# Two more split products, quarter products begun ahead of the half product in front of them, and one more bias sum added by transfers, in a two-layer cross-attention kernel

## The chip, the cores and the metric

The kernel runs on one core of one Trainium2 chip. Its time is the device time of one execution in microseconds; the time given is the median of several. A core has a matrix engine, TensorE (PE in the profile), and three engines for elementwise work: VectorE (DVE), ScalarE (ACT) and GpSimd (POOL). SyncE (SP) issues most of the DMA transfers. Each engine has its own queue of instructions and works through it in order; semaphores make one engine wait for another. PE writes its results to banks of PSUM, a small memory from which ACT and DVE fetch them; all else is in SBUF.

## What is computed

Two layers of cross-attention, all in float32. The queries come from x (8 sequences of 100 tokens of 1024), the keys and values of both layers from one context (8 times 1444 rows of 512). Cut to what matters:

```
# layer 0
Q = x @ Wq + bq ; K = ctx @ Wk + bk ; V = ctx @ Wv + bv
w = softmax(Q @ K.T / sqrt(1024), over the 1444 context rows)
x = x + (w @ V) @ Wo + bo
# layer 1, with weights of its own
q = x @ Wq + bq ; k = ctx @ Wk + bk ; v = ctx @ Wv + bv
w = softmax(q @ k.T / sqrt(1024), over the 100 tokens)
y = w @ v + x
out = layer_norm(y) * gamma + beta
```

## The kernel before

**Products of weights.** Keys and values are never made. Since Q·Kᵀ = x·(Wq·Wkᵀ)·ctxᵀ plus terms of the biases, the kernel first multiplies weights with weights (`weight_products`, L318): Wq·Wkᵀ of layer 0 ("qk0", 1024 to 512), then Wv·Wo of layer 0 ("vo0"), and after the queries of layer 0 Wq·Wkᵀ of layer 1 ("qk1"). `queries(layer)` (L584) multiplies these by x and gives the queries in the context's 512 features: "g0" and "g1". The stages in PE's order are qk0, vo0, g0, qk1, the scores (`s`, L786) and weighted sums of context rows (`A`, L757) of layer 0, the projection "o" by Wv·Wo, g1, scores and sums of layer 1, the projection by Wv, and the layer norm.

**Seven products.** Each of these matrix products is made in the way of Strassen and Winograd: both operands are cut into quarters (A11, A12, A21, A22 and B11 to B22), sums of them are formed on DVE (S1 to S4, T1 to T4), and seven half-size products take the place of eight. The seven are written to banks called X, Z, Y and W: X = A11·B11, Z = A12·B21, Y = S1·T1, then X += S2·T2, W = A22·T4, then X += S3·T3 with S3 = A11 − A21 and T3 = B22 − B12 (its matmuls, taken one at a time, are "V" in the code), and last Y += S4·B22 with S4 = A12 − S2. Between these, `put` copies a bank into the result (on ACT) and `add` adds a bank to it (on DVE). S3, T3 and S4 are written over A21, B12 and A12, so each such sum must wait until the last reader of the old contents is done.

**Inner products.** `inner_product` (L252) makes one of the seven in the same way once more, as seven quarter products in tiles named `.._x`, `.._z`, `.._y`, `.._w`. It forms four sums at once (S1, T1, A21 −, B12 −), and then two more sums behind each of the first two quarter products; later quarters read these. Before the change the products "w" (W) and "q" (the last one, Y += S4·B22) of vo0 and of qk1 are made so, and "w" of g0 and of g1; in qk0 none is.

**What sets the order.** PE's instructions keep the order of the program text (`manual_schedule`, L66). DVE's do so only where `vector.in_order` is set; elsewhere a scheduler orders them, as it does for ACT, except where `keep_in_program_order` is called. In vo0 and qk1 quarters of "w" alternate with pieces of V: after each quarter comes an eighth of V. After the loop comes the rest of V, then `add(1, 0, X)` and `add(1, 1, X)`, four additions of 128x512 from PSUM on DVE, and then all seven quarters of q.

**Bias sums.** The biases of keys, queries and values enter as sums over the rows of a weight matrix, each row scaled by an element of the bias (`accumulate`, L354). Where the rows are 1024 wide this is done for vo0 (bv) and qk1 (bk) by `transferred_sum` (L505): ACT scales the eight chunks into eight tiles (L510), and seven DMA transfers that add what they move to what lies at their destination (L514, issued by POOL) sum them up in three levels. In qk0 the sum for bk is made on DVE, by one scaling and seven multiply-adds of 128x1024. Readers of these sums are `block_sums` (a transpose and a reduction on DVE), called for qk0 within vo0 by `between`.

**Buffers.** Rows of the weights lie in `unit` tiles (ten, loaded by SP, released when the last product that reads them is done); `row` and `wT` tiles have three buffers each, `gT` three, and the three `prob` tiles stay.

Of the kernel before, what the change touches and what calls it, by code (L numbers as in the profile page):

```python
# [25 lines left out]
F32 = mybir.dt.float32  # L26
# [29 lines left out]
def two_layer_cross_attention(ctx: ExitStack, tc: tile.TileContext, a: dict, out: bass.AP):  # L56
# [26 lines left out]
    def weight_rows(name):  # L83
        return work.tile([P, MC * T + QD * (-(-T // QD)) - T], F32, tag="wT", name=name, bufs=3)

# [166 lines left out]
    def inner_product(name, lhs, rhs, nb, width, t, put, add):  # L252
# [18 lines left out]

        combine(S1, A21, A22, ALU.add)
        combine(T1, B12, B11, ALU.subtract)
        combine(A21, A11, A21, ALU.subtract)
        combine(B12, B22, B12, ALU.subtract)
# [4 lines left out]
        def steps():  # L280
            X = bank(f"{name}_x")
            product(X, A11, B11, True)
            put(0, 0, X)
            combine(B11, B22, T1, ALU.subtract)
            combine(A11, S1, A11, ALU.subtract)
            yield
            Z = bank2(f"{name}_z")
            product(Z, A12, B21, True)
            add(0, 0, Z)
            combine(B21, B21, B11, ALU.subtract)  # L290
            combine(A12, A12, A11, ALU.subtract)
            yield
            Y = bank(f"{name}_y")
            product(Y, S1, T1, True)
            put(1, 1, Y)
            yield
            product(X, A11, B11, False)
            put(0, 1, X)
            yield
            W = bank2(f"{name}_w")  # L300
            product(W, A22, B21, True)
            put(1, 0, W)
            yield
            product(Y, A12, B22, False)
            add(0, 1, Y)
            yield
            product(X, A21, B12, False)
            add(1, 1, X)
            add(1, 0, X)
            yield  # L310
# [7 lines left out]
    def weight_products(name, left, right, l_width, r_width, scaled, between=None):  # L318
# [35 lines left out]
        def accumulate(side):  # L354
            for v, of in scaled:
# [5 lines left out]
                if width == E and name != "qk0":  # L361
                    accs[v] = transferred_sum(f"{name}_{v}", srcs)
                    continue
                if width == E:
                    acc = row(f"{name}_{v}")
                else:
                    acc = work.tile([P, L], F32, tag="half", name=f"{name}_{v}", bufs=1)
# [67 lines left out]
        product(X, A11, B11, True)  # L435
        put(0, 0, X)
        combine(T1, B12, B11, ALU.subtract)
        if name == "qk0":
# [11 lines left out]
            product(W, A22, T4, True)  # L450
            put(1, 0, W)
        else:
# [3 lines left out]
            if not early:  # L456
                accumulate(1)
# [3 lines left out]
        put(1, 1, Y)  # L461
        if name != "qk0":
            vector.in_order = True
# [4 lines left out]
        S2 = S1  # L468
        if name != "qk0":
            combine(T4, B21, T2, ALU.subtract)  # L470
        combine(B12, B22, B12, ALU.subtract)
        product(X, S2, T2, False)
        put(0, 1, X)
        if name == "qk0":
            accumulate(0)
        combine(A21, A11, A21, ALU.subtract)
        if name == "qk0":
            combine(A12, A12, S2, ALU.subtract)
            product(X, A21, B12, False)
            add(1, 0, X)  # L480
            add(1, 1, X)
            product(Y, A12, B22, False)
            add(0, 1, Y)
        else:

            V = half_steps(X, A21, B12, False, nb, rh)
            t = work.tile([P, LC, GT], F32, tag="gT", name=f"{name}_t", bufs=3).rearrange("p c t -> p (c t)")
            for n, _ in enumerate(inner_product(f"{name}_w", A22, T4, nb, rh, t[:, :768], *parts(1, 0))):
                run(islice(V, 2 * nb // 4))
                if n == 2:  # L490
                    combine(A12, A12, S2, ALU.subtract)
                    add(0, 1, Y)
                elif n == 3:
                    _, more = parts(0, 1)
                    Q = inner_product(f"{name}_q", A12, B22, nb, rh, t[:, 768:1536], more, more)
                    if between:
                        between()
            run(V)
            add(1, 0, X)
            add(1, 1, X)  # L500
            run(Q)
            vector.in_order = False
        yield dst, [accs[v] for v, _ in scaled]

    def transferred_sum(name, srcs):  # L505

        tiles = [row(f"{name}_{n}") for n in range(2)] + [weight_rows(f"{name}_{n}")[:, :E] for n in range(2, 5)]
# [76 lines left out]
    def queries(layer, w, u):  # L584
# [41 lines left out]

        def steps():
# [4 lines left out]
            Z = pair("z")  # L632
            product(Z, A12, B21, True)
            vector.in_order = True
            combine(S1, A21, A22, ALU.add)
            combine(T1, B12, B11, ALU.subtract)
            combine(S2, S1, A11, ALU.subtract)
            combine(T2, B22, T1, ALU.subtract)
            vector.in_order = False
            yield  # L640
            vector.in_order = True
            add(0, 0, Z)
            combine(A21, A11, A21, ALU.subtract)
            combine(T3, B22, B12, ALU.subtract)
            Y = pair("y")
            product(Y, S1, T1, True)
            put(1, 1, Y)
            combine(T1, B21, T2, ALU.subtract)
            combine(A12, A12, S2, ALU.subtract)
# [6 lines left out]
            t = unit(f"g{layer}_w_t")  # L656
            V = half_steps(X, A21, T3, False, nb, GT)
            for _ in inner_product(f"g{layer}_w", A22, T1, nb, GT, t, *parts(1, 0)):
                next(V)
# [5 lines left out]
            product(Y, A12, B22, False)  # L665
# [426 lines left out]
    for n in range(5):  # L1092
        next(steps)
        if n == 0:
            kb1 = [key_bias_sums(f"kb1_{g}", g * GT, (g + 1) * GT, wqbk1) for g in range(B // G)]
# [60 lines left out]
```

## Time and profile before

| | us |
|---|---|
| Median of 3 runs | 639.41 (639.32 to 640.49) |
| The profiled execution | 639.97 |
| Its span | 638.2 |
| PE's busy time in it | 625.4 |
| VectorE's | 467.0 |
| ScalarE's | 157.2 |
| GpSimd's | 92.9 |

The span is what the hardware profiler saw between the first and the last instruction; the execution is 1.77 us longer. The granted clock of TensorE was 0.996 of full speed in the mean. Where a timeline is shown below, a line gives the start, the time up to the end of the last of a run of like instructions, the engine, the line of the program, the operation, what is written and read, the shape, and the number of instructions. What is in brackets is the time for which the engine had been idle, and who ended it. Ends on PE are modelled and overlap the next start, so times of products are taken from start to start. A float32 matmul of the program appears as two records.

The same page cuts the span into 40 slices of 16 us. Its rows on VectorE, on the granted clock and on the DMA engines, in tenths, are:

```profile
DVE  2993699976883797766655579539786659898886
...
PEclk9999999999999999999999999999999999999998
DMA  8948875015779888999965306156898890599002
```

The four stages of the change lie in slices 0 to 11 (qk0, vo0, g0 and qk1, up to 188.9 us) and in slices 24 to 27 (g1, from 385.8 to 433).

### The profile page before, as it was taken

What the parts mean: (1) busy time and instruction counts of PE and PEld (TensorE: products, weight loads), DVE (VectorE), ACT (ScalarE), POOL (GpSimd) and SP (SyncE); (2) the same over time, 40 slices, a digit from 0 to 9 for tenths busy, and PEclk for the clock granted to TensorE, in tenths of its full rate; (3) what the DMA queues carried; (4) which work ended last, traced back from release to release, by engine and by line L of the source; (5) the groups of instructions that cost most, each with busy time, mean ns of one, the idle gap of its engine ahead of it and who ended that gap; (6) DMA issues with size and microseconds to landing.
All of it is one profiled execution on the core that took longest, in us unless ns stands there. A gap on an engine that the chain in (4) does not pass through costs nothing.

```text
span 638.2 us, 10286 instructions
## 1 busy us (share of the span) xinstructions
PE 625.4 (98%) x4064; PEld 527.6 (83%) x4064; DVE 467.0 (73%) x912; ACT 157.2 (25%) x369; POOL 92.9 (15%) x124
## 2 busy tenths in 40 slices
PE   9999998999999999999999999999999999999994
PEld 8886465678985999999998655656999999999992
DVE  2993699976883797766655579539786659898886
ACT  1012410105203344223330000213432340325301
POOL 3000210001300000000000001007211220454054
PEclk9999999999999999999999999999999999999998
DMA  8948875015779888999965306156898890599002
GB/s 274 356 161 306 164 214 195 0 47 99 151 229 388 293 304 295 324 310 320 305 221 184 111 1 230 46 171 207 274 309 296 309 321 34 194 323 338 29 19 85
DMA packets 50933, 134.64 MB, mean 211 GB/s; under 512 B 4226, under 2 KB 8578, under 8 KB 50886
## 3 DMA queue, kind: packets, MB, share of 16 engines
q1 hardware_dynamic: 46792, 120.85, 55.5%
q0 software_dynamic: 3696, 12.68, 8.4%
q8 instruction: 32, 0.52, 0.3%
q10 hardware_dynamic: 398, 0.47, 0.2%
q14 instruction: 15, 0.12, 0.1%
HBM read 123.36 MB, written 3.28 MB: 198 GB/s over the span
## 4 chain that ended last, share of the span: by engine, by line
PE 91%; DVE 6%; issue 1%; POOL 1%; POOLq 0%; ACT 0%; DVEq 0%
PE s L786 25%; PE A L757 24%; PE qk_x L160 6%; PE g_x L160 5%; PE o_x L160 5%; PE g_y L160 3%; PE qk_y L160 3%; PE o_y L160 3%; DVE vo L93 3%; PE qk_z L160 2%; PE g_z L160 2%; PE o_w L160 2%; PE o_z L160 2%; DVE qk L93 2%; PE vo_x L160 1%
## 5 line engine op out<-in xcount | busy, mean ns | idle before, releaser
L757 PE MATMUL A<-w,c 120*128 120x100 f32 (+1 forms) x1536 | 247.7, 265 | 0.0
L757 PEld LDWEIGHTS A<-w,c 120*128 120x128 f32 (+1 forms) x1536 | 215.9, 190 | 0.8
L93 DVE STREAM_TRANSPOSE w<-prob 32x384 f32<-32x384 f32 (+1 forms) x256 | 143.6, 561 | 35.1 <-ACT prob L798 15.7
L786 PE MATMUL s<-cT,g1T 128*100 128x131 f32 (+2 forms) x592 | 122.9, 296 | 0.3 <-DVE g1T L93 0.3
L786 PE MATMUL s<-cT,g0T 128*100 128x131 f32 (+2 forms) x592 | 122.7, 296 | 0.0
L786 PEld LDWEIGHTS s<-cT,g1T 128*100 128x100 f32 x592 | 78.3, 167 | 9.3 <-DVE g1T L93 1.2
L786 PEld LDWEIGHTS s<-cT,g0T 128*100 128x100 f32 x592 | 78.3, 167 | 8.3
L798 ACT ACTIVATE prob<-s,c 100x393 f32<-100x393 f32 (+2 forms) x64 | 35.1, 561 | 114.4 <-PE s L786 114.1
L908 ACT ACTIVATE w<-w,negmax 120x100 f32<-120x100 f32 (+1 forms) x96 | 34.8, 365 | 82.3 <-DVE negmax L93 82.3
L818 DVE TENSOR_REDUCE maxima<-prob 100x1 f32<-100x394 f32 (+3 forms) x32 | 16.5, 528 | 25.5 <-ACT prob L798 25.3
L1105 POOL DMA_DIRECT2D wv<-in_L_xattn_Wv x1 | 0.8, 772 | 204.9 <-PE o_x L160 204.9
L160 PE MATMUL qk_x<-qk 128*128 128x256 f32 x128 | 29.9, 385 | 0.0
L927 POOL TENSOR_TENSOR part<-w 120x500 f32<-120x500 f32 x8 | 10.9, 1363 | 112.9 <-DVE rstd L1002 28.6
L160 PEld LDWEIGHTS qk_x<-qk 128*128 128x128 f32 x128 | 23.9, 194 | 3.2 <-ACT qk L409 0.2
L93 DVE TENSOR_TENSOR xT<-xT,o_x 128x400 f32<-128x400 f32 (+1 forms) x32 | 16.0, 541 | 6.4 <-PE o_x L160 6.1
L600 ACT ACTIVATE g1T<-g_x,k 128x400 f32<-128x400 f32 x4 | 2.4, 594 | 64.0 <-PE g_x L160 63.8
L908 ACT ACTIVATION_READ_ACCUMULATOR w<-w,negmax 120x1 f32 (+1 forms) x96 | 18.0, 187 | 0.0
L1007 POOL TENSOR_TENSOR z<-z,vectors 100x1024 f32<-100x1024 f32 x7 | 16.5, 2360 | 8.2 <-ACT z L1006 8.2
L985 PE MATMUL z<-ident,xT 128*100 128x128 f32 x64 | 16.3, 273 | 0.0
L93 DVE TENSOR_TENSOR w<-w,rtotal 120x400 f32<-120x400 f32 (+1 forms) x24 | 15.6, 650 | 0.7
L1006 ACT ACTIVATE z<-z,rstd 100x1024 f32<-100x1024 f32 x7 | 8.0, 1150 | 31.9 <-POOL rstd L1003 31.9
L989 DVE SCALAR_TENSOR_TENSOR z<-vectors,r,z 100x512 f32<-100x512 f32 x16 | 11.8, 741 | 4.9 <-PE z L985 4.8
(309 smaller groups left out, 932.5 us busy)
## 6 DMA issues: line engine op xcount, KB each, us to landing
cT<-in_ctxT SPq DMA_DIRECT2D x64, 722.0 KB, 6.4
c<-in_ctx SPq DMA_DIRECT2D x48, 768.0 KB, 8.2
c<-in_ctx SPq DMA_DIRECT2D x16, 512.0 KB, 6.8
vo<-in_L_xattn_Wo SPq DMA_DIRECT2D x8, 512.0 KB, 5.9
qk<-in_L_xattn_WqT SPq DMA_DIRECT2D x8, 512.0 KB
qk<-in_L_xattn_WqT SPq DMA_DIRECT2D x15, 256.0 KB, 5.8
c<-in_ctx SPq DMA_DIRECT2D x16, 224.0 KB, 5.7
xT<-in_xT SPq DMA_DIRECT2D x2, 1600.0 KB
```

What stands on the lines that cost most here:

```text
L93: ins = getattr(nc.vector, op)(*args, **kw)
L160: nc.tensor.matmul(banks[n // per][:, n % per * width : (n % per + 1) * width], lhs[i][:, n * P : (n + 1) * P], rhs[i], start=(fresh and i ...
L757: nc.tensor.matmul(ps[:, k * T : (k + 1) * T], c[m // CQ][:r, m % CQ, k * P : (k + 1) * P], w[:r, m, :], start=(m == 0 and k == 0), stop=( ...
L786: nc.tensor.matmul(banks[n // per][:T, cuts[n] - o : cuts[n + 1] - o], q[:, k, t0 : t0 + T], cT[k][:, cuts[n] : cuts[n + 1]], start=(k == ...
L798: nc.scalar.activation(p[:, part], ps[:T, : part.stop - part.start], AF.Identity, bias=key_bias[layer][:T, b : b + 1], scale=SCALE,)
L818: nc.vector.tensor_reduce(maxima[:, n : n + 1], p[:, part], AX.X, ALU.max)
L908: nc.scalar.activation(w[:r, m0 + m, :], w[:r, m0 + m, :], AF.Exp, bias=negmax[:r, m : m + 1], accum_out=total[:r, m : m + 1])
L927: add(part, w[:MR, 0:5, :], w[:MR, 5:10, :], ALU.add)
L985: nc.tensor.transpose(ps[:T, e * P : (e + 1) * P], xT[:, 4 * j + e, b * T : (b + 1) * T], ident)
L989: nc.vector.scalar_tensor_tensor(z[:, half], bv1[j][:T], s["r"], ps[:T, :], ALU.mult, ALU.add)
L1006: nc.scalar.activation(z, z, AF.Copy, scale=rstd)
L1007: nc.gpsimd.tensor_tensor(z, z, beta[:T], ALU.add)
```

## The change

In **qk0** the bias sum for bk is made by `transferred_sum` too, with other tiles (three `row`, one `wT`, one `gT`, three `prob`), ahead of the copy of W. The last product becomes an inner product "q".

In **qk0, vo0 and qk1** q's first quarter product is issued before the last part of V: in qk0 after half of V, in the others before V's last eighth. The four additions of X go from before q to behind its fifth quarter product. B12 − and, in vo0, A21 − are formed earlier, before T2. In vo0 ACT's scalings for bv go ahead of the copy of X, and DVE keeps the program's order from there on.

In **g1** the product Z becomes an inner product "z", behind Y instead of ahead of it; S4 is written over A11 and the room of T3 serves as room for z's sums. In g0 S4 is formed ahead of T4. `inner_product` gets an argument for where its right-hand sums go. The call of the key bias sums of layer 1 comes four steps later in the text.

```diff
@@ -83,6 +83,9 @@
     def weight_rows(name):
         return work.tile([P, MC * T + QD * (-(-T // QD)) - T], F32, tag="wT", name=name, bufs=3)
+    def wide_sums(name):
+        return work.tile([P, LC, GT], F32, tag="gT", name=name, bufs=3).rearrange("p c t -> p (c t)")
     class Vector:
@@ -249,7 +252,8 @@
         add(0, 1, Y)
         yield
-    def inner_product(name, lhs, rhs, nb, width, t, put, add):
+    def inner_product(name, lhs, rhs, nb, width, t, put, add, right=None):
@@ -269,10 +273,13 @@
         B11, B21, B12, B22 = quarters(rhs, width)
         S1, T1 = room(lhs, t[:, : 2 * h * P]), room(rhs, t[:, 2 * h * P : 2 * h * P + 2 * w])
+        T2, T3, T4 = B11, B12, B21
+        if right:
+            T1, T2, T3, T4 = right
         combine(S1, A21, A22, ALU.add)
         combine(T1, B12, B11, ALU.subtract)
         combine(A21, A11, A21, ALU.subtract)
-        combine(B12, B22, B12, ALU.subtract)
+        combine(T3, B22, B12, ALU.subtract)
         def product(ps, left, right, fresh):
             half_product([ps], left, right, fresh, h, w)
@@ -281,30 +288,30 @@
             X = bank(f"{name}_x")
             product(X, A11, B11, True)
             put(0, 0, X)
-            combine(B11, B22, T1, ALU.subtract)
+            combine(T2, B22, T1, ALU.subtract)
             combine(A11, S1, A11, ALU.subtract)
             yield
             Z = bank2(f"{name}_z")
             product(Z, A12, B21, True)
             add(0, 0, Z)
-            combine(B21, B21, B11, ALU.subtract)
+            combine(T4, B21, T2, ALU.subtract)
             combine(A12, A12, A11, ALU.subtract)
             yield
             Y = bank(f"{name}_y")
             product(Y, S1, T1, True)
             put(1, 1, Y)
             yield
-            product(X, A11, B11, False)
+            product(X, A11, T2, False)
             put(0, 1, X)
             yield
             W = bank2(f"{name}_w")
-            product(W, A22, B21, True)
+            product(W, A22, T4, True)
             put(1, 0, W)
             yield
             product(Y, A12, B22, False)
             add(0, 1, Y)
             yield
-            product(X, A21, B12, False)
+            product(X, A21, T3, False)
             add(1, 1, X)
             add(1, 0, X)
             yield
@@ -358,13 +365,10 @@
                 width = (l_width, r_width)[side]
                 first = 0 if side == 0 else l_width
                 srcs = [(units[h][:, first : first + width], cols[v][:, h : h + 1]) for h in range(EC)]
-                if width == E and name != "qk0":
-                    accs[v] = transferred_sum(f"{name}_{v}", srcs)
+                if width == E:
+                    accs[v] = transferred_sum(f"{name}_{v}", srcs, name == "qk0")
                     continue
-                if width == E:
-                    acc = row(f"{name}_{v}")
-                else:
-                    acc = work.tile([P, L], F32, tag="half", name=f"{name}_{v}", bufs=1)
+                acc = work.tile([P, L], F32, tag="half", name=f"{name}_{v}", bufs=1)
                 accs[v] = acc
                 for h, (src, by) in enumerate(srcs):
                     if h == 0:
@@ -433,7 +437,10 @@
         X = pair("x")
         product(X, A11, B11, True)
+        if name == "vo0":
+            accumulate(1)
         put(0, 0, X)
+        vector.in_order = name == "vo0"
         combine(T1, B12, B11, ALU.subtract)
         if name == "qk0":
@@ -448,63 +455,70 @@
             accumulate(1)
             W = pair("w")
             product(W, A22, T4, True)
+            accumulate(0)
             put(1, 0, W)
         else:
             combine(S1, A21, A22, ALU.add)
             Z = pair("z")
             product(Z, A12, B21, True)
-            if not early:
-                accumulate(1)
             accumulate(0)
         Y = pair("y")
         product(Y, S1, T1, True)
         put(1, 1, Y)
+        vector.in_order = name != "qk0"
+        combine(B12, B22, B12, ALU.subtract)
+        if name == "vo0":
+            combine(A21, A11, A21, ALU.subtract)
         if name != "qk0":
-            vector.in_order = True
             T2, T4 = B11, B21
             combine(T2, B22, T1, ALU.subtract)
             add(0, 0, Z)
         combine(S1, S1, A11, ALU.subtract)
         S2 = S1
+        if name != "vo0":
+            combine(A21, A11, A21, ALU.subtract)
         if name != "qk0":
             combine(T4, B21, T2, ALU.subtract)
-        combine(B12, B22, B12, ALU.subtract)
         product(X, S2, T2, False)
         put(0, 1, X)
+        vector.in_order = True
+        V = half_steps(X, A21, B12, False, nb, rh)
+        t = wide_sums(f"{name}_t")
+        _, more = parts(0, 1)
+        def last():
+            combine(A12, A12, S2, ALU.subtract)
+            add(0, 1, Y)
+            return inner_product(f"{name}_q", A12, B22, nb, rh, t[:, 768:1536], more, more)
         if name == "qk0":
-            accumulate(0)
-        combine(A21, A11, A21, ALU.subtract)
-        if name == "qk0":
-            combine(A12, A12, S2, ALU.subtract)
-            product(X, A21, B12, False)
-            add(1, 0, X)
-            add(1, 1, X)
-            product(Y, A12, B22, False)
-            add(0, 1, Y)
+            run(islice(V, 2 * nb))
+            Q = last()
         else:
-            V = half_steps(X, A21, B12, False, nb, rh)
-            t = work.tile([P, LC, GT], F32, tag="gT", name=f"{name}_t", bufs=3).rearrange("p c t -> p (c t)")
             for n, _ in enumerate(inner_product(f"{name}_w", A22, T4, nb, rh, t[:, :768], *parts(1, 0))):
                 run(islice(V, 2 * nb // 4))
-                if n == 2:
-                    combine(A12, A12, S2, ALU.subtract)
-                    add(0, 1, Y)
-                elif n == 3:
-                    _, more = parts(0, 1)
-                    Q = inner_product(f"{name}_q", A12, B22, nb, rh, t[:, 768:1536], more, more)
+                if n == 3:
+                    Q = last()
                     if between:
                         between()
-            run(V)
-            add(1, 0, X)
-            add(1, 1, X)
-            run(Q)
-            vector.in_order = False
+        next(Q)
+        run(V)
+        run(islice(Q, 4))
+        add(1, 0, X)
+        add(1, 1, X)
+        run(Q)
+        vector.in_order = False
         yield dst, [accs[v] for v, _ in scaled]
-    def transferred_sum(name, srcs):
-
-        tiles = [row(f"{name}_{n}") for n in range(2)] + [weight_rows(f"{name}_{n}")[:, :E] for n in range(2, 5)]
+    def transferred_sum(name, srcs, first):
+        if first:
+            tiles = [row(f"{name}_{n}") for n in range(3)] + [weight_rows(f"{name}_3")[:, :E]]
+            tiles.append(wide_sums(f"{name}_4")[:, :E])
+        else:
+            tiles = [row(f"{name}_{n}") for n in range(2)] + [weight_rows(f"{name}_{n}")[:, :E] for n in range(2, 5)]
         tiles += [t[:, :E] for t in prob]
         for t, (src, by) in zip(tiles, srcs):
             tc.keep_in_program_order(nc.scalar.activation(t, src, AF.Copy, scale=by))
@@ -624,45 +638,68 @@
         def product(banks, lhs, rhs, fresh):
             half_product(banks, lhs, rhs, fresh, nb, GT)
+        t = unit(f"g{layer}_t")
+        def inner(n, lhs, rhs, put, add, right=None):
+            return inner_product(f"g{layer}_{n}", lhs, rhs, nb, GT, t, put, add, right)
         def steps():
             X = pair("x")
             product(X, A11, B11, True)
             put(0, 0, X)
             yield
-            Z = pair("z")
-            product(Z, A12, B21, True)
+            S3, S4 = A21, A12
+            if layer == 0:
+                Z = pair("z")
+                product(Z, A12, B21, True)
+            vector.in_order = layer == 0
+            combine(S1, A21, A22, ALU.add)
             vector.in_order = True
-            combine(S1, A21, A22, ALU.add)
             combine(T1, B12, B11, ALU.subtract)
             combine(S2, S1, A11, ALU.subtract)
-            combine(T2, B22, T1, ALU.subtract)
-            vector.in_order = False
-            yield
-            vector.in_order = True
-            add(0, 0, Z)
-            combine(A21, A11, A21, ALU.subtract)
-            combine(T3, B22, B12, ALU.subtract)
+            if layer == 0:
+                combine(T2, B22, T1, ALU.subtract)
+                vector.in_order = False
+                yield
+                vector.in_order = True
+                add(0, 0, Z)
+            combine(S3, A11, A21, ALU.subtract)
+            if layer == 0:
+                combine(T3, B22, B12, ALU.subtract)
             Y = pair("y")
             product(Y, S1, T1, True)
             put(1, 1, Y)
+            if layer:
+                vector.in_order = False
+                yield
+                vector.in_order = True
+                S4 = A11
+                combine(S4, A12, S2, ALU.subtract)
+                _, more = parts(0, 0)
+                room = [[T3[0][:, n, :].rearrange("p (i t) -> p i t", i=2)] for n in range(4)]
+                Z = inner("z", A12, B21, more, more, room)
+                combine(T2, B22, T1, ALU.subtract)
+                run(Z)
+                combine(T3, B22, B12, ALU.subtract)
+            else:
+                combine(S4, A12, S2, ALU.subtract)
             combine(T1, B21, T2, ALU.subtract)
-            combine(A12, A12, S2, ALU.subtract)
             vector.in_order = False
             yield
             product(X, S2, T2, False)
             put(0, 1, X)
             yield
             vector.in_order = True
-            t = unit(f"g{layer}_w_t")
-            V = half_steps(X, A21, T3, False, nb, GT)
-            for _ in inner_product(f"g{layer}_w", A22, T1, nb, GT, t, *parts(1, 0)):
+            V = half_steps(X, S3, T3, False, nb, GT)
+            for _ in inner("w", A22, T1, *parts(1, 0)):
                 next(V)
             run(V)
             add(1, 0, X)
             add(1, 1, X)
             vector.in_order = False
             yield
-            product(Y, A12, B22, False)
+            product(Y, S4, B22, False)
             add(0, 1, Y)
             yield
@@ -1089,10 +1126,8 @@
         run(steps)
     gT[1], steps = queries(1, wqk1, u1)
-    for n in range(5):
-        next(steps)
-        if n == 0:
-            kb1 = [key_bias_sums(f"kb1_{g}", g * GT, (g + 1) * GT, wqbk1) for g in range(B // G)]
+    run(islice(steps, 5))
+    kb1 = [key_bias_sums(f"kb1_{g}", g * GT, (g + 1) * GT, wqbk1) for g in range(B // G)]
     *_, key_bias[1] = key_biases("c1", kb1, bqbk1)
     vectors = [unit(f"vectors_{j}") for j in range(2)]
     gamma, beta = (t[:, :E] for t in vectors)
```

## The prediction

> **What bounds the kernel now.** I read the page first, then what ended TensorE's waits, then the timelines of the stages that the change touches.
>
> ```profile
> PE 625.4 (98%) x4064; PEld 527.6 (83%) x4064; DVE 467.0 (73%) x912; ACT 157.2 (25%) x369; POOL 92.9 (15%) x124
> ...
> PE 91%; DVE 6%; issue 1%; POOL 1%; POOLq 0%; ACT 0%; DVEq 0%
> ```
>
> TensorE (PE) is busy 98% of the span and carries 91% of the chain of waits. So the kernel gets faster in two ways only: PE is given less to do, or one of its few waits goes. VectorE (DVE) carries 6% of the chain. All waits of PE are these:
>
> ```profile
> PE vo_q_x L160 <- DVE vo L93: 2.0, 1, 2.0
> PE qk_q_x L160 <- DVE qk L93: 1.1, 1, 1.1
> PE warm L105 <- DVE ones L102: 1.1, 1, 1.1
> PE s L786 <- DVE g1T L93: 0.3, 1, 0.3
> ```
>
> (Total, times, longest, in us.) The first two lie where the change moves work: in the inner product "q" of vo0 and of qk1. The chain in order of time is on DVE from 74.91 to 98.84 in vo0 and from 170.58 to 184.81 in qk1.
>
> **1. The split in qk0 (PE).** The last product Y += A12·B22 was one half product and becomes seven quarter products. PE's timeline in qk0, and q of qk1, which has the same sizes:
>
> ```profile
> 46.62 7.07 PE L160 MATMUL qk_y<-qk 128*128 128x256 f32 x32
> 53.53 0.28 PE L551 MATMUL bb_ps<-bbs,ones 128*128 128x2 f32 x2
> ...
> 180.82 1.05 PE L160 MATMUL qk_q_x<-qk 128*128 128x128 f32 x8
> 181.72 1.06 PE L160 MATMUL qk_q_z<-qk 128*128 128x128 f32 x8
> 182.61 1.06 PE L160 MATMUL qk_q_y<-qk_t 128*128 128x128 f32 x8
> 184.81 1.16 PE L160 MATMUL qk_q_x<-qk 128*128 128x128 f32 x8 [1.14 <-DVE qk L93]
> ```
>
> Starts give the pace: 53.53 − 46.62 = 6.91 us for 32 records (0.216 each); 182.61 − 180.82 = 1.79 for two quarters, so 0.893 for 8 records (0.112 each). Seven quarters are 6.25 us: **0.66 saved**.
>
> A rule speaks against this. The Trainium skill, "TensorE: Matmul & The Clock Gate", section "Back-to-back issue gap", has sustained spacings of some 81 ns at a width of 128 and 131 ns at 512: a narrower matmul keeps most of its cost, since its weight load stays. Interpolated (my estimate) a width of 256 would take 98 ns, so 56 records of 128 against 32 of 256 would be 4.5 to 3.1, 45% dearer; 6.91 would become 10.0, and this part would cost 3.1 us instead of saving 0.66. The rows say 0.112 against 0.216: here half the width is nearly half the time. The row decides. With the rule, the sum below would be 1.5 us instead of 5.3.
>
> Who must be in time? q's preparation on DVE (A12 −= S2, two adds of Y, the sums of the split: some 5 us) must end before q's first quarter at 43.1, the middle of V. In before, DVE's in-place A12 ran only from 41.88, because the bias sum of bk (one TENSOR_SCALAR and seven SCALAR_TENSOR_TENSOR of 128x1024, pace 1.2 us, 9 us between 27.9 and 40.7) lay among it. These 9 us leave DVE; that is the cover. Nobody on PE waited for them, so they are worth nothing by themselves. If the preparation were late, PE would wait as long.
>
> **2. The bias sum by transfers.** ACT gets 8 scalings of 128x1024, at a pace of 1.04 us: some 8.5 us, about 21.5 to 30. ACT stood idle 12.36 us before 25.16, and next works at 32.06. Queued behind them is the put of W (25.16 in before), now near 30; the bank it frees is next written by q's second quarter at 44. Cost 0. Then POOL issues seven adding transfers of 512 KB. This is how those of vo0 went:
>
> ```profile
> 63.80 0.92 POOL L514 DMA_DIRECT2D vo_L_xattn_bv<-vo_L_xattn_bv  x1 [57.96 <-ACT vo_L_xattn_bv L510]
> ...
> 80.00 0.85 POOL L514 DMA_DIRECT2D vo_L_xattn_bv<-prob  x1 [6.50 <-issue]
> 85.03 0.85 POOL L514 DMA_DIRECT2D vo_L_xattn_bv<-vo_L_xattn_bv  x1 [4.18 <-issue]
> ```
>
> The first scaling was at 61.3, the last issue at 85.03, and each lands 5.2 to 6.9 us after its issue: 29 us for the whole. In qk0 that is 21.5 to 50 or 54, of which 32 to 48 is the slice in which the page has the DMA engines at 4 tenths (9 and 8 in the slices beside it). The sum's reader, the transpose at 91.72, comes 38 us later. Cost 0. vo0's own chain needs the same tiles: its last scalings wait for qk0's sixth transfer (45 to 50) and for Wo's last rows.
>
> SP's queue: Wv/Wo units 6 and 7 are loaded into rows that q now reads to its end; they issue near 51.8 and 52.9 instead of 48.54 and 50.27, land near 59 to 60, and vo0's second product needs them at 63.4 and 65.1: 4 us of slack. Behind them on SP are only qk1's rows, needed at 139. If they landed over 4 us later than that, PE would wait as long; I take 0.
>
> **3. vo0.** Before:
>
> ```profile
> 95.86 1.03 PE L160 MATMUL vo_q_y<-vo_t 128*128 128x256 f32 x4
> 98.84 1.13 PE L160 MATMUL vo_q_x<-vo 128*128 128x256 f32 x4 [1.96 <-DVE vo L93]
> ...
> 102.61 0.29 PE L532 MATMUL u<-u_sums,same 128*128 128x16 f32 x2
> ```
>
> and DVE's timeline there:
>
> ```profile
> 95.11 2.48 DVE L93 TENSOR_TENSOR vo<-vo,vo_x 128x512 f32<-128x512 f32 x4
> ...
> 97.83 0.76 DVE L93 TENSOR_TENSOR vo<-vo,vo_t 128x256 f32<-128x256 f32 x2
> ```
>
> The four adds of X (2.48 us) stood in DVE's queue ahead of the sums that q's second x quarter needs. They go behind five quarters of q. Also B12 −= (four 128x512 at a pace of 0.60: 2.4 us) and A21 −= (four 128x256 at 0.335: 1.4) leave the stretch after Y. So DVE is relieved of 6.3 us against a stall of 1.96 plus quarters stretched by 0.33 (98.84 to 102.61 is 3.77, four at 0.861 are 3.44). What is late next: q's second x quarter has its sums at 95.6 on before's clock, where PE asks at 96.05: 0.45 to spare. From w's first quarter at 81.22 to 102.61 PE took 21.39; seven quarters of w, seven of q and V (worth eight) at 0.861 are 18.94. **2.45 saved.** The moved-ahead scalings put the put of X behind ACT's queue, to about 62; X is next written at 73. Cost 0.
>
> **4. g0.** DVE arrives with 1.8 us less ahead of it, PE is 3.1 earlier; T1 = B21 − T2, now behind A12 −=, is ready 0.85 before its use. Lower end 0, upper 0.4 if the adds of vo0's X run late: I take 0.
>
> **5. qk1.** The same four adds (181.21, 2.48 us) moved. 167.66 to 188.77 is 21.11; fourteen quarters at 0.893 and V at 6.91 are 19.41: **1.70 saved**. The late adds now stand near the first scores, whose banks wait for them with 0.3 to 0.6 to spare.
>
> **6. g1.** Product Z (16 records of 400) becomes seven quarters:
>
> ```profile
> 391.19 5.54 PE L160 MATMUL g_z<-xT,qk 128*128 128x400 f32 x16
> 396.56 0.83 PE L160 MATMUL g_y<-g_t,g_s 128*128 128x400 f32 x2
> ...
> 407.31 0.84 PE L160 MATMUL g_w_x<-g_t,qk 128*128 128x200 f32 x4
> 407.99 0.83 PE L160 MATMUL g_x<-g_t,qk 128*128 128x400 f32 x2
> ```
>
> 5.37 becomes 7 × 0.673 = 4.71: 0.66. But here no V lies between the quarters, so PE asks for sums every 0.67 us while DVE's 128x400 operations take 0.49 each. Laid out by hand, three operands arrive within 0.15 us of their use. Ends: 0.66 and 0.36; I take **0.5**. The new sums (5.1 us) run in DVE's gaps among the o0 adds (idle 7.9 us between 361 and 386). The 0.34 wait of the scores stays.
>
> **Sum.** 0.66 + 2.45 + 1.70 + 0.5 = 5.3 us. All stages behind are PE's and shift. The profiled execution took 639.97 (span 638.2, 1.77 around): 634.7, span 632.9. The runs' median, 639.41, lies 0.56 below it: **634.1 us**, 0.83% less. A difference within 0.2% (1.3 us) cannot be told from none.
>
> **Rivals.**
> (a) The waits go only in part. For: PE comes 3 to 5 us earlier while DVE's work is hardly less, and five margins above are under 0.9 us. Against: each was counted with its releaser. If DVE is 0.4 late at each of five places, 2.0 us come back: 636.1.
> (b) Only the splits count: DVE's stalls of vo0 and qk1 merely move to another quarter, since the adds still must be made before the next stage. For: DVE has no idle time there. 639.41 − 1.2 = 638.2. Against: PE's next stage does not read the adds of X at once.
> (c) Slower: ACT's in-order queue in vo0. If qk0's adding transfers, now beside the Wv/Wo loads, land late, vo0's scalings wait, the put of X behind them with them, and PE's second write of X at 73 stands still. From 62 to 73 are 11 us of cover; past it every us is a us, and from 16.3 us late the kernel is slower: at 18 us, 641.1. For: the last two transfers of vo0 waited 6.50 and 4.18 us to issue, with the DMA engines at 8 and 7 tenths. Against: most of qk0's chain lies in the slice of 4 tenths, and it would have to last half as long again.
>
> **Numbers.** Forecast 0.62 (own range 633.6 to 635.3); (a) 0.22; (b) 0.06; (c) 0.05; 0.05 for what I haven't seen. Low end: the g1 end of 0.66 and half a us more of short gaps, 633.5. High end: (a) with 0.5 per place, 636.7. Faster 0.92, same 0.03 (part of (b)), slower 0.05.
>
> **What would show it.** Steps 3 and 5: vo_q_x and qk_q_x gone from PE's waits, or below 0.3. Step 1: q of qk0 in 6.25 us, without a wait at its first quarter. Step 6: seven quarters of g_z from first to last in 4.7 to 5.0. Steps 2 and (c): ACT's put of vo_x before 65, no wait of PE at the third product of vo0. Wrong it would be if PE's list of waits has new entries on DVE in g0, or at the first scores, of over 1 us together, or if a quarter of qk0's q takes over 0.95 us.

## The result, and the profile after

| | before | after |
|---|---|---|
| Median | 639.90 (20 runs, 639.22 to 640.78) | 636.24 (20 runs, 634.94 to 642.20) |
| Ratio | | 0.9962 (95% interval 0.9946 to 0.9979) |
| The profiled execution, its span | 639.97, 638.2 | 638.23, 636.1 |

The change makes the kernel faster by some 2.4 us by the ratio and 3.7 by the medians, where 5.3 were forecast: the median of 636.24 is 2.1 us above the forecast of 634.1. Its runs lie over 7 us where those of before lie over 1.6. From the page of after:

```profile
PE 623.6 (98%) x4100; PEld 529.5 (83%) x4100; DVE 469.7 (74%) x942; ACT 165.9 (26%) x377; POOL 98.9 (16%) x131
...
q0 software_dynamic: 4704, 16.35, 11.3%
...
PE 93%; DMA 4%; DVE 1%; POOL 1%; issue 1%; POOLq 0%; ACT 0%; DVEq 0%; SPq 0%
```

DVE's share of the chain went from 6 to 1%. A share that was not there is now there: DMA, 4%, which counts the whole way of two transfers (24 us) and not only PE's wait for them. All waits of PE:

```profile
PE vo_z L163 <- DMA vo<-in_L_xattn_Wo: 2.8, 1, 2.8
PE warm L108 <- DVE ones L105: 1.1, 1, 1.1
PE s L823 <- DVE g1T L96: 0.3, 1, 0.3
```

The waits in vo_q_x and qk_q_x are gone, as forecast. In their place PE waits in vo0's second product for the last row of Wo. PE's timeline there, and the chain of waits in order of time (start, length, what):

```profile
52.82 0.28 PE L565 MATMUL bb_ps<-bbs,ones 128*128 128x2 f32 x2
...
59.91 5.31 PE L163 MATMUL vo_z<-vo 128*128 128x512 f32 x12
67.98 1.96 PE L163 MATMUL vo_z<-vo 128*128 128x512 f32 x4 [2.76 <-DMA vo<-in_L_xattn_Wo]
```

```profile
53.08 14.77 DMA vo<-in_L_xattn_Wo
```

And GpSimd's queue, where the last of qk0's adding transfers is followed by two of vo0's:

```profile
56.81 0.85 POOL L528 DMA_DIRECT2D qk_L_xattn_bk<-qk_L_xattn_bk  x1 [7.91 <-issue]
57.35 2.08 POOL L528 DMA_DIRECT2D vo_L_xattn_bv<-vo_L_xattn_bv  x2
```

The row was issued at 53.08, about as forecast (52.9), and landed after 14.77 us instead of the 6 to 7 that the forecast gave it. PE wanted it at 65.05. Stage by stage, from the starts in PE's timelines (us; "fourth" is the changed kernel in a later run, of 634.88 us, without this wait):

| | before | after | fourth | forecast of the difference |
|---|---|---|---|---|
| start to the end of qk0 | 53.53 | 52.82 | 52.52 | −0.66 |
| vo0 | 49.08 | 49.64 | 46.64 | −2.45 |
| g0 | 37.20 | 37.22 | 37.22 | 0 |
| qk1 | 48.96 | 47.26 | 47.26 | −1.70 |
| g1 up to the sums of c | 31.60 | 31.30 | 31.31 | −0.5 |

So the shortfall of the profiled span is vo0's, 3.0 us, and a little g1's. The fourth run has a span of 632.8, where the forecast had 632.9. That they agree so closely is in part luck: of the 1.01 us that the fourth run saves in qk0, 0.36 come from its first product, which the change does not touch (7.02 us there, 7.38 in before, 7.89 in after_again).

A small term lies outside the span. The execution is 2.11 us longer than its span, where before's was 1.77 and the forecast kept 1.77. In the seven traces of this document that have qk0's transfers and do not hold back vo0's, this difference is 2.10 to 2.14; in the eleven others it is 1.76 to 1.84. Why was not found.

### The profile page after: what moved, and what is told of

Its sections match the earlier page's. It is cut to its first block, busy times and chain, and to the rows that moved or that the text cites. A ratio compares the mean times of both kernels' runs of the same rounds, so it can differ in the third digit from the quotient of the medians.

```text
span 636.1 us, 10422 instructions
## 1 busy us (share of the span) xinstructions
PE 623.6 (98%) x4100; PEld 529.5 (83%) x4100; DVE 469.7 (74%) x942; ACT 165.9 (26%) x377; POOL 98.9 (16%) x131
## 3 DMA queue, kind: packets, MB, share of 16 engines
q0 software_dynamic: 4704, 16.35, 11.3%
## 4 chain that ended last, share of the span: by engine, by line
PE 93%; DMA 4%; DVE 1%; POOL 1%; issue 1%; POOLq 0%; ACT 0%; DVEq 0%; SPq 0%
PE s L823 25%; PE A L794 24%; PE qk_x L163 6%; PE g_x L163 5%; PE o_x L163 5%; DMA vo<-in_L_xattn_Wo 4%; PE g_y L163 3%; PE o_y L163 3%; PE qk_y L163 2%; PE qk_z L163 2%; PE vo_x L163 2%; PE o_w L163 2%; PE o_z L163 2%; PE qk_w L163 1%; PE vo_y L163 1%; PE z L1022 1%
## 5 line engine op out<-in xcount | busy, mean ns | idle before, releaser
L528 POOL DMA_DIRECT2D qk_L_xattn_bk<-qk_L_xattn_bk x8 | 6.9, 863 | 102.5 <-ACT qk_L_xattn_bk L524 80.8
```

Of the source, the lines that this page charges most:

```text
L528: nc.gpsimd.dma_start(out=tiles[i], in_=tiles[i + n], accum_op=ALU.add)
```

## The experiments

Five theories came up. A: qk0's seven adding transfers fill the DMA engines, so Wo's rows land late. B: q of qk0 holds Wo's buffers, so the rows are issued late. C: vo0's own first adding transfers, issued earlier than before, run beside the last row. D: the spread is one chip's. E: the place of the four additions of X carries all the gain of vo0 and qk1. Each run was compared with before on the same chip (medians 640.0 to 640.3).

**1. Other ways to sum, held transfers, the product whole.** Four edits. In pool_adds GpSimd adds in place of qk0's transfers; in vo_sums_late the pair of tiles that vo0's transfers add first needs the last row of Wo, so that all of vo0's transfers are held until it has landed; in qk0_whole qk0's last product has no q; before_sums is before with qk0's bias sum alone made by transfers.

```diff
 # pool_adds, for qk0
-nc.gpsimd.dma_start(out=tiles[i], in_=tiles[i + n], accum_op=ALU.add)
+nc.gpsimd.tensor_tensor(tiles[i], tiles[i], tiles[i + n], ALU.add)
 # vo_sums_late, for vo0, with the transfers kept in program order
+order = [tiles[k] for k in (0, 7, 2, 3, 4, 5, 6, 1)]
-nc.gpsimd.dma_start(out=tiles[i], in_=tiles[i + n], accum_op=ALU.add)
+nc.gpsimd.dma_start(out=order[i], in_=order[i + n], accum_op=ALU.add)
 # qk0_whole
-Q = last()
+product(Y, A12, B22, False)
+add(0, 1, Y)
```

> The changed kernel with qk0's seven adding transfers replaced by seven GpSimd additions of 128x1024 (some 2.4 us each, the row of the 100x1024 addition in the tail); ACT's scalings, the split and vo0's own transfers stay. Theory A (qk0's adding transfers fill the DMA engines, 18 us of all 16 of them, so that the last Wo rows land 9 to 15 us after their issue): no wait of PE in vo_z, Wo's landings back near 6 us, runs within 1.5 us of each other, median 634.9 to 635.4. Theory B (the rows are late because q of qk0 holds their buffers, and they are issued 2.5 us later): the wait stays at over 1 us, median 636 to 638. Theory C (vo0's own first adding transfers, now issued before the last rows have landed, compete with them): the wait stays, perhaps longer, since nothing holds these transfers back any more.

> The changed kernel with vo0's adding transfers paired so that the first to be issued needs the last row of Wo: none of vo0's runs beside the loads, while qk0's seven stay. Theory A with qk0's transfers alone as the cause: the wait stays over 1 us in most runs, median 636 or more. Theory C: the wait is gone, median 634.9 to 635.4. If both share it (two transfers of 2.6 us each are some 5 us of the engines, more than the wait of 2.8): wait 0 to 1, median near 635.5. Theory B: no change, 636.2.

> The changed kernel with qk0's last product whole again (no q there), so that rows of Wo go out near 48.5 and 50.3 as before, while the adding transfers stay. Theory A: the engines are full anyway, so the last row lands at most 1 us earlier; the wait stays between 2 and 3.5, median 636.5 to 637.5 (0.66 of the split lost). Theory B: the wait is gone, median 635.6.

> The kernel before with qk0's bias sum by scalings and adding transfers and nothing else. Theory A: Wo's rows land 9 us after issue instead of 5.9, PE waits in vo_z in many runs, the median is 0.5 to 3 us above before and the runs spread over 3 us or more. Theories B and C (neither the held buffers nor the early scalings of vo0 are there): no wait, time as before within 0.3 us.

| | median (runs) | ratio (95%) | wait in vo_z |
|---|---|---|---|
| pool_adds | 649.38 (648.81 to 650.05) | 1.0143 (1.0129 to 1.0157) | none |
| vo_sums_late | 635.94 (635.25 to 636.67) | 0.9934 (0.9920 to 0.9947) | 0.31 |
| qk0_whole | 636.15 (635.21 to 636.71) | 0.9935 (0.9923 to 0.9948) | none |
| before_sums | 640.53 (639.64 to 642.01) | 1.0004 (0.9995 to 1.0013) | none |

pool_adds tells nothing of the three theories: another wait, of 12.5 us for DVE, stands in front. Its waits, and DVE's timeline:

```profile
PE qk_x L163 <- DVE qk_s L96: 12.5, 1, 12.5
```

```profile
29.39 2.58 DVE L96 TENSOR_TENSOR qk<-qk,qk 128x256 f32<-128x256 f32 x1
31.89 2.83 DVE L96 SCALAR_TENSOR_TENSOR qk_L_xattn_bq<-qk,L_xattn_bq,qk_L_xattn_bq 128x512 f32<-128x512 f32 x1
```

These two take 0.42 and 0.75 in after. While GpSimd adds (2.4 to 2.8 us each), each DVE instruction that starts between 26.6 and 37.2 takes 2.5 to 2.9 us.

before_sums speaks against A alone: the transfers are all there, Wo's rows land 9.5 us after issue in the median instead of 5.9, and yet PE waits for none, and its 13 runs lie over 2.4 us where those of before beside them lie over 3.1. Its last row is issued at 52.66, vo0's own transfers go out only from 63.65, and PE asks 0.6 us later than in after.

qk0_whole does not test B as it was meant to. The last row goes out at 52.73 there, hardly earlier than in after, and at 52.66 in before_sums: neither has a q in qk0, and before issues it at 50.64. So most of the late issue comes with the transfers, and q's hold on the buffers is worth some 0.4 us at most. In the one trace of qk0_whole the wait is gone, though Wo's rows land 9.8 us after issue in the median.

vo_sums_late has the last row land after 11.72 us instead of 14.77, which takes all but 0.31 of the wait. That alone does not show C, since the changed kernel itself does as well in its fourth run, with vo0's two transfers issued as early as in after. GpSimd's and ACT's timelines there (the scaling of the last row starts as it lands, 11.5 us after its issue at 52.77):

```profile
57.44 2.08 POOL L528 DMA_DIRECT2D vo_L_xattn_bv<-vo_L_xattn_bv  x2
64.28 1.15 ACT L524 ACTIVATE prob<-vo,L_xattn_bv 128x1024 f32<-128x1024 f32 x1 [2.54 <-DMA vo<-in_L_xattn_Wo]
```

What speaks for C is the spread, in part 5.

**2. The price of an adding transfer.** copies: the changed kernel with plain copies in qk0, which leaves out the sum for the key bias.

```diff
-nc.gpsimd.dma_start(out=tiles[i], in_=tiles[i + n], accum_op=ALU.add)
+nc.gpsimd.dma_start(out=tiles[i], in_=tiles[i + n])   # qk0 only
```

> The changed kernel with qk0's seven transfers as plain copies instead of adding ones: the same bytes, order and waits; the sum of the scaled rows for layer 0's key bias is left out with that. Theory A by occupancy of the engines: an adding transfer takes 2.6 us of all 16 engines, a plain one of 512 KB at the 400 GB/s of the loads 1.3; the backlog is 9 us shorter, Wo's rows land 6 us after issue, no wait in vo_z, runs within 1.5 us, median 635.3 to 635.9. Theory A by bytes alone (the adding costs nothing): Wo's landings stay at 9 us, the wait and the spread stay.

635.53 (634.88 to 637.62), ratio 0.9925 (0.9911 to 0.9939). The share of the 16 DMA engines and the GB/s from 32 to 48 us, in 40 slices, with the queues' shares (packets, MB, share), of after and then of copies:

```profile
DMA  9999999999999999999999999999999999998999
GB/s 228 228 232 232 236 236 268 236 242 236 228 228 248 225 360 423 422 436 382 420 225 261 241 241 236 266 251 302 246 302 246 271 241 282 246 277 225 420 415 440
...
q0 software_dynamic: 545, 1.97, 61.7%
```

```profile
DMA  9999999999999999999998531007889899869968
GB/s 400 396 419 392 400 364 413 398 421 368 394 384 420 394 440 379 440 389 420 394 430 338 215 154 51 31 31 266 271 184 307 353 394 256 241 189 230 189 205 312
...
q0 software_dynamic: 502, 1.80, 28.2%
```

Adding, 1.97 MB held the engines for 0.617 × 16 = 9.9 us: 200 GB/s, 2.6 us for 512 KB. Copying, 1.80 MB took 4.5 us: 400 GB/s, 1.3 us. In the slices in which transfers add, the whole core moves some 225 to 300 GB/s; between them 360 to 440. So A's price is right. Its cure does not always work: with the backlog shorter, vo0's own transfers went out at 52.67 instead of 57.35, beside the last row, which landed after 14.26 us; the profiled run waited 2.2 us in vo_z and is the one of 637.62, while the other four lie at 634.88 to 635.54. That fits C, in one trace.

**3. Which part brings the gain.** On the base of vo_sums_late, one part undone at a time: adds_first, not_ahead.

```diff
 # adds_first
 next(Q)
 run(V)
-run(islice(Q, 4))
 add(1, 0, X)
 add(1, 1, X)
 run(Q)
 # not_ahead
-next(Q)
 run(V)
-run(islice(Q, 4))
+run(islice(Q, 5))
```

> The version with vo0's adding transfers held until the last rows have landed (635.94 in its own runs), with the four additions of X put back ahead of the rest of q in qk0, vo0 and qk1. By the prediction's steps 3 and 5 (DVE is short by 2.48 us less a margin of 0.45 in vo0 and of 1.7 in qk1): PE waits 2.0 us for DVE in vo_q_x and 0.8 in qk_q_x, none in qk0, +2.8: 638.7. Rival: what leaves the stretch after Y (B12, A21) is enough, and the additions' place does not matter: no wait, 635.9.

> The same held version with q's first quarter product issued behind V instead of ahead of its last part, all else kept. By the margins of the prediction: in vo0 DVE's sums get 0.86 us less, 0.4 more than the margin: a wait of 0.4; in qk1 none; in qk0 half of V (3.5 us) no longer covers the first sums, a wait of 0 to 0.5. Sum +0.4 to +0.9: 636.3 to 636.8. Rival (beginning ahead is what carries the gain, so that the old waits of 2.0 and 1.1 come back): 638.5 to 639.

adds_first: 639.93 (638.80 to 642.39), ratio 0.9997 (0.9987 to 1.0007). Its waits:

```profile
PE vo_q_w L163 <- DVE vo L96: 1.9, 1, 1.9
PE qk_q_w L163 <- DVE qk L96: 1.2, 1, 1.2
```

vo0 takes 49.38 us there, 0.26 of it a wait for Wo's row (49.08 in before), and qk1 48.95 (48.96). The waits are those that were expected, in another quarter (1.9 and 1.2, against 2.0 and 0.8). With the additions back, nothing is left of the gain of vo0 and qk1. not_ahead, expected at 636.3 to 636.8: 635.48 (635.12 to 635.96), ratio 0.9928 (0.9916 to 0.9941), qk0 52.38, qk1 47.28, no wait in any q. Its profile has a wait of 1.17 us in vo_z, for a row issued at 55.03 (so holding vo0's transfers does not rule the wait out); without that vo0 takes 47.03, against 46.88 in vo_sums_late without its 0.31. So beginning ahead brings nothing that can be told here.

**4. Without any transfer.** lean is before with one more line. lean_z adds the change's queries of layer 1; lean_q adds the split in qk0, behind V, with the bias sum left on DVE; lean_q2 also keeps DVE in program order from vo0's first sum on.

```diff
 # lean, in vo0 and qk1
 run(V)
+run(islice(Q, 5))
 add(1, 0, X)
 add(1, 1, X)
 run(Q)
 # lean_q, in qk0
-combine(A12, A12, S2, ALU.subtract)
 product(X, A21, B12, False)
+vector.in_order = True
+combine(A12, A12, S2, ALU.subtract)
+add(0, 1, Y)
+...
+Q = inner_product(f"{name}_q", A12, B22, nb, rh, t[:, 768:1536], more, more)
+run(islice(Q, 5))
 add(1, 0, X)
 add(1, 1, X)
-product(Y, A12, B22, False)
-add(0, 1, Y)
+run(Q)
 # lean_q2
+vector.in_order = name == "vo0"
 combine(T1, B12, B11, ALU.subtract)
```

> The kernel before with one line more: in vo0 and qk1 the four additions of X stand behind five quarters of q instead of ahead of q. No added transfers, no split more, no earlier B12, A21 or first quarter. Theory E (the place of these additions carries the whole gain of vo0 and qk1): the waits in vo_q_x and qk_q_x are gone, vo0 takes 46.7 to 47.2 instead of 49.1 and qk1 47.3 instead of 49.0, ratio 0.9935 to 0.9945 (636.0 where before is 640.0), runs over 1.5 us at most. Rival (the earlier B12 and A21 are needed too, as the prediction had it): a wait of 1 to 2 us stays in vo0, 638.

> The version lean with the change's queries: product Z of layer 1 as an inner product. By the trace of the changed kernel (5.08 us instead of 5.37): 0.3 less than lean, ratio 0.993 to 0.994.

> The version lean_z with qk0's last product split too, but behind V and with the bias sum left on DVE. If the 9 us of the bias sum need not leave DVE for that: another 0.4 to 0.7 less, ratio 0.992 to 0.9932, no wait of PE on DMA since no transfer is added. If DVE is late (its sums for q would be ready near 48, where the third quarter asks at 48.4): waits of up to 1 us in qk_q, no gain over lean_z.

> The version lean_z: no transfers added, so no wait on DMA in any run: 635.2 to 636.3, all runs within 1.2 us, below the changed kernel in the mean by 0.5 us or more.

> The version lean_q with DVE held to the program's order from vo0's first sum on, so that no sum of vo0 (1.88 us there) goes ahead of the sums of qk0's q. If these three sums were what made q wait 1.02: no wait in qk_q, 0.4 to 0.7 below lean_z: 634.8 to 635.5. If DVE is late by its bias sum anyway: a wait of 0.5 or more stays, and the time is that of lean_z or above.

| | median (runs) | ratio (95%) |
|---|---|---|
| lean | 636.41 (635.51 to 636.55) | 0.9939 (0.9927 to 0.9951) |
| lean_z | 635.80 (635.23 to 636.25) | 0.9931 (0.9919 to 0.9943) |
| lean_z_again | 636.21 (635.03 to 636.39) | 0.9930 (0.9919 to 0.9942) |
| lean_q | 636.61 (636.23 to 637.04) | 0.9947 (0.9934 to 0.9960) |
| lean_q2 | 635.04 (634.89 to 635.67) | 0.9918 (0.9905 to 0.9931) |

E holds: one line gives 3.7 us, vo0 46.78 and qk1 47.28, with no wait of PE on DVE in either, though B12 and A21 are formed as late as in before. PE in lean: the start of vo0, the quarter that waited in before, and the start of g0:

```profile
54.06 0.28 PE L552 MATMUL bb_ps<-bbs,ones 128*128 128x2 f32 x2
...
97.25 1.03 PE L160 MATMUL vo_q_x<-vo 128*128 128x256 f32 x4
...
100.84 0.29 PE L533 MATMUL u<-u_sums,same 128*128 128x16 f32 x2
```

lean_q lost by three sums of vo0 that the scheduler put ahead of q's; with the order kept, the wait is gone. DVE and PE of lean_q, and PE of lean_q2:

```profile
47.14 1.88 DVE L93 TENSOR_TENSOR vo_s<-vo 128x512 f32<-128x512 f32 x3
48.95 0.41 DVE L93 TENSOR_TENSOR qk<-qk,qk_q_x 128x256 f32<-128x256 f32 x1
```

```profile
50.15 1.16 PE L160 MATMUL qk_q_x<-qk 128*128 128x128 f32 x8 [1.02 <-DVE qk L93]
```

```profile
46.65 1.05 PE L160 MATMUL qk_q_x<-qk 128*128 128x128 f32 x8
...
52.91 0.28 PE L563 MATMUL bb_ps<-bbs,ones 128*128 128x2 f32 x2
```

In lean_q2 the seven quarters take 6.26 us, with the 9 us of the bias sum still on DVE. lean_q2 is below both kernels, 0.8% under before.

**5. The spread.** The changed kernel three more times, and the held version beside the last.

> The changed kernel once more, beside the others on the same chip. Theory A with the held buffers (adding transfers make the last rows of Wo land late by a varying amount, 0 to 7 us past their use): median 636 to 639, runs over a range of 3 us or more, a wait of PE in vo_z in the profile of any slow run. Theory D (the spread was that chip's, not the kernel's): runs within 1.5 us.

> The changed kernel a third time, beside the three. Theory A with the held buffers: anything between 635.5 and 639, with runs above 637 where the last rows of Wo land late; theory D (the spread was one chip's): 635.7 with runs within 1 us.

> The changed kernel beside the three below. As before: median 635.7 to 637.2, with single runs up to 643 where the last row of Wo lands late.

> The changed kernel with vo0's adding transfers held until the last row of Wo has landed, on the same chip. Theory C (these two transfers beside the row decide): no run above 637, median 635.3 to 636.2. Theory A alone (the backlog from qk0's seven decides): it spreads like the changed kernel, single runs at 639 and more.

| | median (runs) | runs above 637 |
|---|---|---|
| after_again | 635.75 (635.67 to 636.11) | 0 of 5 |
| after_third | 637.11 (635.58 to 643.20) | 7 of 14 |
| after_fourth | 637.69 (634.52 to 641.06) | 7 of 12 |
| held_again | 635.91 (635.49 to 636.68) | 0 of 5 |

The spread comes with qk0's transfers together with the rest of the change. Without them (part 4) each set lies within 1.4 us, 24 runs in all, and lean_q and lean_q2 have q in qk0 and no wait in vo_z, so B alone is not the cause either.

D falls: with the 20 runs of the result, 22 of 51 lie above 637, in three of four sets, on two chips at least. C is supported by counting: of the 15 runs of vo_sums_late, not_ahead and held_again, which hold vo0's transfers, none lies above 636.7. after_fourth and held_again ran on the same chip, 7 of 12 against 0 of 5; on the chip of not_ahead the changed kernel (after_again) had none above 637 either. qk0_whole, which does not hold them, had none in five, so C is likely and not shown to be the only cause.

Why the row comes late in one execution and not in the next was not found. In after and in the fourth run qk0's and vo0's last issues differ by 0.1 us, and from 57.4 to 66 the queue of adding transfers held 45 and 46% of the engines; the row landed at 67.85 in one and near 64.3 in the other. In the fourth run that is 0.5 us before PE asks for it, so there too hardly any slack was left.

## Why the prediction was right and wrong

- **Step 1** (split in qk0): right in the time, 6.26 us for seven quarters in lean_q2 and 6.25 forecast. The rule on narrow matmuls, which would have made it 3.1 us dearer, does not hold for these rows. Wrong was that it takes the 9 us of the bias sum off DVE to give q cover: in lean_q2 they stay, q stands behind V (at 46.65 instead of 43.1) and does not wait. Since not_ahead shows no gain from the earlier place, the transfers were not needed.
- **Step 2 failed**, in its paragraph on SP's queue: "land near 59 to 60, and vo0's second product needs them at 63.4 and 65.1: 4 us of slack ... I take 0." The landing was mis-sized: 14.77 us after issue where some 7 were forecast, so that PE, with no slack left, waited 2.76 us in the profiled execution, nearly all of vo0's 3.0 us of shortfall. The issue times came out right, but not for the reason given: without any q in qk0 the last row goes out at 52.66 and 52.73 (before_sums, qk0_whole). I priced the seven transfers by how long one takes to land and by one slice at 4 tenths, and not by how long it holds the engines. Before's own trace had that number: from 63 to 97 us its queue of adding transfers held the engines for 56.8% of 34 us, 19.3 us for seven, 2.8 each:

```profile
q0 software_dynamic: 1008, 3.67, 56.8%
```

In the profile of before the engines had some 8 us free between 34 and 43, and 4.3 between 59 and 65: less than the 18 to 19 that were added. The page of after agrees: the queue's share rose from 8.4 to 11.3% of the span, 18 us. What makes this long landing come in some executions only stays open.
- Also in step 2 and 3: that vo0's scalings are moved ahead was costed at ACT's queue alone. With them vo0's first adding transfers moved from 63.80 to 57.35, beside the last row (C, likely but not shown to decide).
- **Rival (c)** had the right resource and the wrong victim. The put of X came at 68.99, 7 us later than I had it, and cost nothing, since X is next written at 76.64. The row of Wo was what PE waited for.
- **Steps 3 and 5**: right in size (−2.44 and −1.70 without the wait), wrong in the reason: "DVE is relieved of 6.3 us" counted B12 and A21, which lean shows to be worth 0.14 us at most in vo0 (46.78 against 46.64 in the fourth run). The 2.48 us of additions are the rest. The list of waits shows one cause for both stages, and one line removes it.
- **Step 4**: right, g0 is unchanged.
- **Step 6** (g1): 0.29 instead of 0.5. From the first quarter of z to the next product:

```profile
394.75 0.84 PE L163 MATMUL g_z_x<-xT,qk 128*128 128x200 f32 x4
...
396.94 0.94 PE L163 MATMUL g_z_x<-g_t,qk 128*128 128x200 f32 x4
...
399.83 2.51 PE L163 MATMUL g_x<-g_t,g_s 128*128 128x400 f32 x7
```

5.08 us, outside the 4.7 to 5.0 that I gave: DVE was late by 0.37 in three places, where I had reckoned with 0.16.
- **Rival (a)** (DVE late at five places, 636.1) is near the median by chance: the list of waits has no new one on DVE, and where DVE was late, between g1's quarters, it cost 0.37 in all. **Rival (b)** did not happen.

## What to carry to other kernels

Price a transfer by the time for which it holds the DMA engines, from its queue's share in the trace, and add that up against the free time before the next load that an engine needs; a landing time and an average in tenths do not tell it. When a stall has one named cause, undo that cause alone first: here one line moved gave most of the gain, and the rest of the change opened a new wait. Where a transfer is moved earlier, look at which load it now runs beside. And where runs spread, one trace of each kind does not tell the cause: count runs.

## What the runs showed of the hardware

- An adding transfer of 512 KB from SBUF to SBUF held the 16 engines for 2.6 us, a copy of the same bytes for 1.3.
- A wait of PE cost more than its length in one run. In the third run of the changed kernel PE waited 2.19 us in vo_z, and the four matmul records behind it took 3.49 us from start to start where after's took 1.80. The windows of this run (us, busy times, PEclk, DMA share, GB/s) and its timeline:

```profile
68.00:72.00 4.00, 4.00 (x6) 1.70 (x7) 4.00 (x9) 2.03 (x3) 0.00 (x0) 0.57 1.05 264
```

```profile
67.97 3.65 PE L163 MATMUL vo_z<-vo 128*128 128x512 f32 x4 [2.19 <-DMA vo<-in_L_xattn_Wo]
71.46 4.03 PE L163 MATMUL vo_y<-vo_s 128*128 128x512 f32 x9
```

The granted clock (the column behind the five engines) was 0.57 in these 4 us, and 1.00 in the same stretch of after, whose wait was longer (2.76). The Trainium skill, "TensorE: Matmul & The Clock Gate", section "What's actually happening", has the gate judge PE's activity in free-running windows of some 3.4 us, which fits a wait that costs the clock in one run and not in another. It names an idle window of that length as what lowers the clock; this wait was shorter. The lower clock added 1.7 us to this run, of 639.82 us; how often that happens, no other trace shows.
- GpSimd's additions held up DVE's: 0.42 became 2.58 us (pool_adds). The skill's "SBUF — State Buffer", section "Who interferes with whom", says that an addition of two SBUF operands on DVE and a GpSimd instruction that reads SBUF take turns at one shared port; the trace agrees.
